# Layer 0 of a four-layer graph network: where x, the row sums and the loads of the adjacency matrix are placed

## The chip, the cores and the metric

The kernel runs on one core of a Trainium2 chip. A core has five engines that run their own instruction streams side by side and wait for each other by semaphores: TensorE (PE, matrix products, with its weight loads listed apart as PEld), VectorE (DVE), ScalarE (ACT), GpSimd (POOL) and SyncE (SP), which here only issues DMA transfers. Transfers are issued from an engine's queue (SP's or ACT's) and are carried out by 16 DMA engines. The metric is the time of one execution on the device in microseconds (us); lower is better.

## The reference, cut to what matters

There are N = 2708 nodes with D = 128 features, x[N, D], and a sparse weighted matrix adj[N, N] stored dense in float32 (29.3 MB). Four layers follow each other; each takes h = relu(layernorm(x)) and adds its output to x.

```
h = max(layernorm(x), 0)
layer 0:  x = x + (adj.T @ h) / adj.sum(axis=0)[:, None]
layer 1:  s, d = h @ Wa.T, h @ Wb.T
          x = x + ln(gelu([h, sum_j gelu(s_i + d_j + b) * adj_ij] @ U.T + u) + h)
layer 2:  x = x + gru(relu((adj @ h) @ W.T + b), h)
layer 3:  x = x + sum over 2 heads of elu(ln(softmax(masked scores) @ hh + h) @ F.T) / 2
```

Layer 1 would need a gelu for each of N x N pairs; the kernel does it only for the entries of adj that are not zero. For this it draws up lists in layer 0, while adj passes through the core.

## The kernel before, in words

*Tiles.* The 2708 rows are cut into 22 row tiles (NT) of 128, the last of 20. Row tiles are taken four at a time (GROUPS: five groups of 4 and one of 2). Columns are cut into 22 blocks (NB) of 124 for the lists.

*Start.* Lines 78 to 82 issue the loads of x from ACT's queue into xs, one transfer per group. `normalise` (L140, called at L157) runs for each group: `moments` (L109) on VectorE takes mean and variance of each row, GpSimd takes the power -1/2 (L119), `factors` (L122) makes one Newton step and the shift on VectorE, and `scale_rows` (L132) writes h on ScalarE. Constants for layer 1 follow (L174 to L191, L199): count, ident_h, before, xb and offdiag.

*Layer 0* (L197 to L258) loops over groups, and in a group over its row tiles:

- The buffer `a4` holds four row tiles; there are two of them, so group g + 2 needs the buffer of group g. Each row tile has a load of its own on SP's queue (L218).
- TensorE multiplies h of the row tile with its six column chunks into six PSUM banks, which collect over all row tiles (L220).
- GpSimd copies the columns near the diagonal into `near` without the diagonal, and the diagonal alone into `dg` (L229 to L232). VectorE sums `dg` into `own` (L235).
- VectorE takes for each of the 22 column blocks the eight largest entries of every row and their positions (L240, L241). These are the lists.
- ScalarE counts the entries of a row as the sum of their signs (L243).
- After a group's row tiles, TensorE transposes them, four 128 x 128 blocks into one PSUM bank (L249, two banks); ScalarE copies the bank to `aT` and sums it (L253: `sums` gives the column sums of adj); SP stores `aT` to a transposed copy of adj in DRAM (L256), which layer 2 and layer 3 read. There are four `aT` buffers.

At the end ScalarE copies the six banks to sumT (L258), and VectorE makes the inverse column sums (L263 to L267).

*What sets the order.* In layer 0 a scheduler orders each engine's instructions; each engine then takes its own strictly in that order, and so does SP with its transfers: a load that waits for a buffer holds back the stores behind it. From layer 1 on the order is written out by hand. Layer 1 opens on VectorE with count_rows (L333), rank (L349), the inverse sums and `enter` (L656), which adds layer 0's result to x.

*Weights.* `load`, `load_columns` and `load_rows` (L87 to L103) issue the weights of layers 1 to 3 from ACT's queue. gate_b and half_b (L276 to L279) are made on VectorE ahead of layer 1; `layer3_weights` (L286) runs in layer 2.

Of the kernel before, what the change touches and what calls it, by code (L numbers as in the profile page):

```python
# [20 lines left out]
F32 = mybir.dt.float32  # L21
BF16 = mybir.dt.bfloat16
AF = mybir.ActivationFunctionType
ALU = mybir.AluOpType
# [36 lines left out]
def listed_layers(ctx: ExitStack, tc: tile.TileContext, x, adj, w, out, flag):  # L61
# [14 lines left out]


    nc.vector.memset(xs[:, NT - 1, :], 0.0)
    for t, k in GROUPS[:-1]:
        nc.scalar.dma_start(xs[:, t : t + k, :], x[t * P : (t + k) * P, :].rearrange("(t p) d -> p t d", p=P))  # L80
    nc.scalar.dma_start(xs[:, FULL - 1, :], x[(FULL - 1) * P : FULL * P, :])
    nc.scalar.dma_start(xs[0:TAIL, FULL, :], x[FULL * P : N, :])

    ident = const.tile([P, P], F32, name="ident")
    make_identity(nc, ident)

    def load(pool, name, shape=None):  # L87
        t = pool.tile(list(shape or w[name].shape), F32, name=name)
        nc.scalar.dma_start(t, w[name])
        return t  # L90

    def load_columns(pool, name):

        k = w[name].shape[0] // P
        t = pool.tile([P, k], F32, name=name)
        nc.scalar.dma_start(t, w[name].rearrange("(k p) -> p k", p=P), allow_slow_non_contiguous=True)
        return t

    def load_rows(pool, name):

        t = pool.tile([P, w[name].shape[0]], F32, name=name)
        nc.scalar.dma_start(t, w[name].partition_broadcast(P))
        return t  # L103


    minus_half = const.tile([P, 8], F32, name="minus_half")
    nc.vector.memset(minus_half, -0.5)

    def moments(src, name, pool=small):  # L109
# [22 lines left out]
    def scale_rows(dst, src, rstd, shift, func):  # L132

        for q in range(len(src)):
            nc.scalar.activation(dst[q], src[q], func, bias=shift[:, q : q + 1], scale=rstd[:, q : q + 1])

    def tiles_of(v, t, k):
        return [v[:, t + q, :] for q in range(k)]

    def normalise(dst, src, t, k, func, name):  # L140

        rows = tiles_of(src, t, k)
        scale_rows(tiles_of(dst, t, k), rows, *factors(*moments(rows, name)), func)
# [10 lines left out]
        n = span(first, k)[1]  # L154
        (copy or nc.vector.tensor_copy)(dst, p[:, 0:n])

    for t, k in GROUPS:  # L157
        normalise(h, xs, t, k, AF.Relu, "n0")

    late = ctx.enter_context(tc.tile_pool(name="late", bufs=1))  # L160
    lists = ExitStack()
# [12 lines left out]
    count = keep.tile([P, P], F32, name="count")  # L174
    nc.gpsimd.iota(count, [[1, P]], base=0, channel_multiplier=0, allow_small_or_imprecise_dtypes=True)
    count_h = keep.tile([P, P], BF16, name="count_h")
    nc.vector.tensor_copy(count_h, count)
    ident_h = keep.tile([P, P], BF16, name="ident_h")
    nc.vector.tensor_copy(ident_h, ident)
    part = keep.tile([P, 1], F32, name="part")  # L180
    nc.gpsimd.iota(part, [[0, 1]], base=0, channel_multiplier=1, allow_small_or_imprecise_dtypes=True)
    before = keep.tile([P, P], BF16, name="before")
    nc.vector.tensor_scalar(before, count, part, None, ALU.is_gt)
    ends4 = keep.tile([P, NB, R], BF16, name="ends4")
    rows_n = keep.tile([P, NT, NB], BF16, name="rows_n")
    ends = keep.tile([P, NT, NB], BF16, name="ends")
# [1 line left out]
    nc.gpsimd.memset(later, 0.0)  # L188
    xb = [keep.tile([P, NB, C], BF16, name=f"xb{q}") for q in range(2)]
    for q in range(2):  # L190
        nc.vector.tensor_copy(xb[q][:, :, 4 * S : 4 * S + R], part.unsqueeze(1).to_broadcast([P, NB, R]))  # L191

# [2 lines left out]
    with tc.tile_pool(name="l0c", bufs=1) as fix:  # L197
        offdiag = fix.tile([P, P], F32, name="offdiag")
        nc.vector.tensor_scalar(offdiag, ident, -1.0, 1.0, ALU.mult, ALU.add)  # L199
        sums = fix.tile([P, NT, len(GROUPS)], F32, name="sums")  # L200
        nc.gpsimd.memset(sums, 1.0)
        with (
            tc.tile_pool(name="l0", bufs=2) as rows,
            tc.tile_pool(name="l0k", bufs=2) as pool,
            tc.tile_pool(name="l0t", bufs=4) as turned,
            tc.tile_pool(name="l0p", bufs=1, space=PSUM) as acc,
        ):
            accs = [acc.tile([P, CH], F32, name=f"acc{c}") for c in range(len(CHUNKS))]
            for gi, (g0, gk) in enumerate(GROUPS):
                i0, iw = span(g0, gk)  # L210
                a4 = rows.tile([P, 4, N], F32, name="a")
                if gk < 4:
                    nc.gpsimd.memset(a4[:, gk - 1, :], 0.0)
                for q in range(gk):
                    n = g0 + q
                    m = size(n)
                    a = a4[:, q, :]
                    nc.sync.dma_start(a[0:m, :], adj[n * P : n * P + m, :])  # L218
                    for ci, (c, cw) in enumerate(CHUNKS):
                        nc.tensor.matmul(  # L220
                            accs[ci][:, 0:cw], h[0:m, n, :], a[0:m, c : c + cw], start=(n == 0), stop=(n == NT - 1)
                        )

                    d0 = n * P
                    b0 = d0 // JB
                    b1 = (d0 + m - 1) // JB
                    c0, c1 = b0 * JB, min((b1 + 1) * JB, N)
                    near = pool.tile([P, 3 * JB], F32, name="near")
                    nc.gpsimd.tensor_copy(near[:, 0 : c1 - c0], a[:, c0:c1])  # L229
                    dg = pool.tile([P, P], F32, name="dg")  # L230
                    nc.gpsimd.tensor_tensor(dg[:, 0:m], a[:, d0 : d0 + m], ident[:, 0:m], ALU.mult)
                    nc.gpsimd.tensor_tensor(  # L232
                        near[:, d0 - c0 : d0 - c0 + m], a[:, d0 : d0 + m], offdiag[:, 0:m], ALU.mult
                    )
                    nc.vector.reduce_sum(own[:, n : n + 1], dg[:, 0:m], AX.X)  # L235
                    for b in range(NB):
                        ab = a[:, b * JB : b * JB + width(b)]
                        if b0 <= b <= b1:
                            ab = near[:, b * JB - c0 : b * JB - c0 + width(b)]
                        nc.vector.max(val[:, n, b, :], ab)  # L240
                        nc.vector.max_index(col[:, n, b, :], val[:, n, b, :], ab)  # L241
                    sign = pool.tile([P, N], BF16, name="sign")
                    nc.scalar.activation(sign, a, AF.Sign, accum_out=total[:, n : n + 1])  # L243
                for j in range(NT):
                    k = size(j)
                    p = bank("p_T")
                    for q in range(gk):
                        m = size(g0 + q)
                        nc.tensor.transpose(  # L249
                            p[0:k, q * P : q * P + m], a4[0:m, q, j * P : j * P + k], ident[0:m, 0:m]  # L250
                        )
                    aT = turned.tile([P, CH], F32, name="aT")
                    nc.scalar.activation(  # L253
                        aT[0:k, 0:iw], p[0:k, 0:iw], AF.Copy, accum_out=sums[0:k, j, gi : gi + 1]
                    )
                    nc.sync.dma_start(adjT[0:k, j, i0 : i0 + iw], aT[0:k, 0:iw])  # L256
            for ci, (c, cw) in enumerate(CHUNKS):
                nc.scalar.copy(sumT[:, c : c + cw], accs[ci][:, 0:cw])  # L258


        deg = fix.tile([P, 3, NT], F32, name="deg")
        dsum, lim, fin = (deg[:, q, :] for q in range(3))
        nc.vector.reduce_sum(dsum, sums, AX.X)  # L263
        nc.vector.reciprocal(inv, dsum)
        nc.vector.tensor_scalar(lim, inv, FMAX, -FMAX, ALU.min, ALU.max)
        nc.vector.tensor_tensor(fin, lim, inv, ALU.is_equal)
        nc.vector.tensor_tensor(inv, lim, fin, ALU.mult)  # L267
# [5 lines left out]
    attn = load_columns(late, "attn")  # L273
    gain1, shift1, gain2, shift2 = (load_columns(late, v) for v in ("g1", "b1", "g2", "b2"))
    gate_b = late.tile([P, 2], F32, name="gate_b")
    nc.vector.tensor_tensor(gate_b, b_ih[:, 0:2], b_hh[:, 0:2], ALU.add)  # L276
    nc.vector.tensor_scalar(gate_b, gate_b, 0.5, None, ALU.mult)
    half_b = late.tile([P, 1], F32, name="half_b")
    nc.vector.tensor_scalar(half_b, b_hh[:, 2:3], 0.5, None, ALU.mult)  # L279


    NX = 2 * D + 4
    w_x = late.tile([P, NX], F32, name="w_x")
    src_w = late.tile([P, 2, P], F32, name="src_w")

    def layer3_weights():  # L286
        nc.vector.tensor_copy(w_x[:, 0 : 2 * D], ff0T)
        for k in range(2):
            p = bank("p_w")[:, 0:2]
            nc.tensor.matmul(p, ff0[:, k, :], attn[:, 2 * k : 2 * k + 2], start=True, stop=True)  # L290
            nc.vector.tensor_copy(w_x[:, 2 * D + k : 2 * D + k + 1], p[:, 1:2])
            nc.vector.tensor_copy(w_x[:, 2 * D + 2 + k : 2 * D + 3 + k], p[:, 0:1])
        for k in range(2):
            nc.vector.tensor_copy(src_w[:, k, :], w_x[:, 2 * D + 2 + k : 2 * D + 3 + k].to_broadcast([P, P]))
# [639 lines left out]
    with (  # L934
# [127 lines left out]
        for g, (t0, k0) in enumerate(GROUPS):  # L1062
            pa = accs.tile([P, CH], F32, tag=f"acc{g % 2}", name="p_agg")
            for j0 in range(0, NT, PIECE):
                aggregate(t0, k0, pa, j0)
            if t0 == 0:
                layer3_weights()
            follow(finish_chunk(t0, k0, pa))
            advance()
        last = RUNS[0]  # L1070
# [486 lines left out]
```

## Time and profile before

| | |
|---|---|
| time, median of 3 runs | 1110.71 us (1109.0 to 1111.08) |
| span of the profiled execution | 1108.1 us, mean granted TensorE clock 0.933 |
| busy: PE, DVE, ACT, POOL | 963.6, 839.4, 504.2, 394.1 us |
| layer 0: first adj load issued, last list entry | 0.7 us, 244.3 us |
| layer 0, 28 to 244 us: busy PE, DVE, ACT, POOL | 178.2, 215.6, 135.3, 27.6 us |
| moved in this stretch | 237 GB/s, DMA share 0.68 |
| layer 1 opens with L656 at | 246.85 us |

How to read the profile lines: a line of the order of time gives start, length, engine, line of the kernel, operation, what it writes and reads with shapes, how many were merged, and in brackets the idle time before it and what ended it. A line of the waits says who waited for whom: total us, number of times, the longest. A line of the stretches gives busy us per engine with the number of instructions, then the granted clock (1.00 is full speed), the DMA share and GB/s. Busy times of TensorE are pipelined matmuls, so they overstate its work. Adding busy times up over the kernel says little here, since its layers have different limits: layer 0 has to be looked at by itself.

### The profile page before, as it was taken

What the parts mean: (1) busy time and instruction counts of PE and PEld (TensorE: products, weight loads), DVE (VectorE), ACT (ScalarE), POOL (GpSimd) and SP (SyncE); (2) the same over time, 40 slices, a digit from 0 to 9 for tenths busy, and PEclk for the clock granted to TensorE, in tenths of its full rate; (3) what the DMA queues carried; (4) which work ended last, traced back from release to release, by engine and by line L of the source; (5) the groups of instructions that cost most, each with busy time, mean ns of one, the idle gap of its engine ahead of it and who ended that gap; (6) DMA issues with size and microseconds to landing.
All of it is one profiled execution on the core that took longest, in us unless ns stands there. A gap on an engine that the chain in (4) does not pass through costs nothing. (4 is left out here: it accounts for less than half of the span.)

```text
span 1108.1 us, 21904 instructions
## 1 busy us (share of the span) xinstructions
PE 963.6 (87%) x7968; PEld 760.1 (69%) x7968; DVE 839.4 (76%) x2948; ACT 504.2 (46%) x1319; POOL 394.1 (36%) x466
## 2 busy tenths in 40 slices
PE   3998887944389999999999979999979999999993
PEld 1455444523389999999898934444468899999772
DVE  5999999997766668676887255655578977997673
ACT  3857556623476666656676521433322200230142
POOL 4111111103385655776566253344310200340132
PEclk9999889755699999999999989999989999999996
DMA  9488978522133222322222056545300000000000
GB/s 361 164 299 281 324 259 288 178 64 68 46 106 102 96 86 90 106 86 101 83 103 80 28 193 209 190 157 198 100 18 1 1 9 1 1 20 1 2 15 14
DMA packets 55298, 125.39 MB, mean 113 GB/s; under 512 B 7414, under 2 KB 19782, under 8 KB 52472
## 3 DMA queue, kind: packets, MB, share of 16 engines
q1 hardware_dynamic: 48590, 121.12, 31.6%
q10 hardware_dynamic: 6590, 2.77, 1.0%
q8 instruction: 64, 1.05, 0.4%
q14 instruction: 54, 0.44, 0.1%
HBM read 77.30 MB, written 30.84 MB: 98 GB/s over the span
## 5 line engine op out<-in xcount | busy, mean ns | idle before, releaser
L838 PE MATMUL att<-hv,wt 128*128 128x129 f32 (+2 forms) x1936 | 240.7, 281 | 9.2 <-DVE wt L806 9.2
L838 PEld LDWEIGHTS att<-hv,wt 128*128 128x128 f32 (+2 forms) x1936 | 221.8, 190 | 26.2 <-DVE wt L806 9.1
L806 DVE SCALAR_TENSOR_TENSOR wt<-row,lift,mask 128x1024 f32<-128x1024 f32 (+5 forms) x176 | 160.0, 939 | 34.2 <-PE att L838 34.2
L423 POOL TENSOR_SCALAR put<-mine,value 128x128 f32<-128x128 bf16 x176 | 147.7, 855 | 72.4 <-DVE mine L339 70.0
L499 PE MATMUL p_m<-s,sel 128*128 128x128 bf16 x1452 | 160.8, 219 | 5.4 <-ACT g L511 5.4
L119 POOL TENSOR_TENSOR n_r<-n_r,minus_half 128x4 f32<-128x4 f32 (+1 forms) x36 | 51.3, 1425 | 316.1 <-DVE n_r L118 305.2
L503 PE MATMUL p_m<-d,cols 124*128 124x128 bf16 (+1 forms) x1452 | 161.0, 219 | 1.4 <-DVE cols L453 1.3
L220 PE MATMUL acc<-a,hs 128*128 128x512 f32 (+2 forms) x264 | 122.3, 599 | 27.6 <-DMA a<-in_adj 18.9
L524 PE MATMUL agg<-put,g 128*128 128x128 f32 (+1 forms) x968 | 135.8, 281 | 0.0
L241 DVE FIND_INDEX8 col<-val,a 128x8 uint16<-128x124 f32 (+1 forms) x441 | 118.6, 280 | 0.0
L959 PE MATMUL p_agg<-a,hs 128*128 128x512 f32 (+2 forms) x264 | 111.5, 564 | 7.7 <-DVE u L572 4.8
L524 PEld LDWEIGHTS agg<-put,g 128*128 128x128 f32 x968 | 118.1, 192 | 0.0
L499 PEld LDWEIGHTS <-sel 128*128 128x128 bf16 x1452 | 103.7, 97 | 10.8 <-issue 7.1
L503 PEld LDWEIGHTS <-cols 124*128 124x128 bf16 (+1 forms) x1452 | 101.8, 97 | 1.9 <-DVE cols L453 1.9
L240 DVE MAX8 val<-a 128x8 f32<-128x124 f32 (+1 forms) x441 | 102.6, 272 | 0.0
L511 ACT ACTIVATE g<-p_m 128x512 f32<-128x512 f32 x132 | 73.0, 553 | 63.6 <-PE p_m L503 63.6
L431 ACT ACTIVATE put<-mine,value 128x128 f32<-128x128 bf16 x308 | 100.5, 390 | 0.0
L220 PEld LDWEIGHTS acc<-a,hs 128*128 128x128 f32 (+1 forms) x264 | 49.7, 209 | 72.2 <-issue 43.4
L249 PEld LDWEIGHTS p_T<-ident,a 128*128 128x128 f32 x484 | 59.0, 146 | 52.8 <-ACT aT L253 25.4
L249 PE MATMUL p_T<-ident,a 128*128 128x128 f32 x484 | 77.7, 293 | 18.3 <-DMA a<-in_adj 10.0
L253 ACT ACTIVATE aT<-p_T 128x512 f32<-128x512 f32 (+2 forms) x132 | 70.9, 541 | 40.0 <-issue 16.3
L959 PEld LDWEIGHTS p_agg<-a,hs 128*128 128x128 f32 (+1 forms) x264 | 48.6, 196 | 56.6 <-issue 55.1
(228 smaller groups left out, 1396.6 us busy)
## 6 DMA issues: line engine op xcount, KB each, us to landing
a<-in_adj SPq DMA_DIRECT2D x21, 1354.0 KB
adjT<-aT SPq DMA_DIRECT2D x105, 256.0 KB
a<-adjT SPq DMA_DIRECT2D x20, 1280.0 KB
spread<-passed SPq DMA_DIRECT2D x22, 704.0 KB
later<-sel SPq DMA_DIRECT2D x22, 616.0 KB
later<-sel SPq DMA_DIRECT2D x22, 82.5 KB
adjT<-aT SPq DMA_DIRECT2D x21, 74.0 KB
a<-adjT SPq DMA_DIRECT2D x4, 370.0 KB
```

Of the source, the lines that this page charges most:

```text
L220: nc.tensor.matmul(accs[ci][:, 0:cw], h[0:m, n, :], a[0:m, c : c + cw], start=(n == 0), stop=(n == NT - 1))
L240: nc.vector.max(val[:, n, b, :], ab)
L241: nc.vector.max_index(col[:, n, b, :], val[:, n, b, :], ab)
L249: nc.tensor.transpose(p[0:k, q * P : q * P + m], a4[0:m, q, j * P : j * P + k], ident[0:m, 0:m])
L423: nc.gpsimd.tensor_scalar(st["put", 0][:, b, :], st["mine"][:, b, :], st["value"][:, b : b + 1], None, ALU.mult)
L431: nc.scalar.activation(st["put", 1][:, b - HP, :], st["mine"][:, b, :], AF.Identity, scale=st["value"][:, b : b + 1])
L499: nc.tensor.matmul(p[:, b - b0, :], st["sel"][:, b, :], s3[:, q, t % 2, :], start=(q == 0), stop=False)
L503: nc.tensor.matmul(p[:, b - b0, :], st["cols"][0:kb, b, :], d3[0:kb, b, q, :], start=False, stop=(q == 2))
L524: nc.tensor.matmul(agg, g[:, b - 4 * k, :], put, start=(b == 0), stop=False)
L806: nc.vector.scalar_tensor_tensor(wt[0:kj, :], row[0:kj, k, c : c + n], lift[0:kj, j, k : k + 1], mask[0:kj, j, c : c + n], op0=ALU.max, op ...
L838: nc.tensor.matmul(banks[s // 3][0:m, s % 3, :], wt[0:kj, q * P : q * P + m], hv[0:kj, j, k, :], start=(v < 2 and s // 3 not in touched), ...
L959: nc.tensor.matmul(pa[:, 0:n], h[0:k, j, :], a[0:k, j - j0, 0:n], start=(j == 0), stop=(j == NT - 1))
```

## The change

The change rearranges layer 0; nothing of what is computed changes.

1. The first four row tiles of x are loaded ahead of adj on SP's queue; the other 18 follow after the second row tile of adj (`load_rest`). All weights go to SP's queue as well.
2. Only the first four tiles are normalised as before. For the others `moments_apart` takes the moments on ScalarE, by a Copy and a Square, each with a sum over its columns, and makes the factors on GpSimd for all 18 tiles together.
3. The sum of the diagonal, `own`, goes from VectorE to ScalarE.
4. Groups 1 to 4 are loaded by one transfer for four row tiles; the first and the last group keep one for each row tile. There are eight `aT` buffers.
5. Constants of layer 1 are made on GpSimd; gate_b and half_b are made later, in layer 2.

It is meant to start VectorE's lists sooner, to leave VectorE nothing but the lists, and to issue fewer transfers.

```diff
-    for t, k in GROUPS[:-1]:
-        nc.scalar.dma_start(xs[:, t : t + k, :], x[t * P : (t + k) * P, :].rearrange("(t p) d -> p t d", p=P))
-    nc.scalar.dma_start(xs[:, FULL - 1, :], x[(FULL - 1) * P : FULL * P, :])
-    nc.scalar.dma_start(xs[0:TAIL, FULL, :], x[FULL * P : N, :])
+    nc.sync.dma_start(xs[:, 0:4, :], x[0 : 4 * P, :].rearrange("(t p) d -> p t d", p=P))
+    def load_rest():
+        for t, k in GROUPS[1:-1]:
+            nc.sync.dma_start(xs[:, t : t + k, :], x[t * P : (t + k) * P, :].rearrange("(t p) d -> p t d", p=P))
...
-    for t, k in GROUPS:
-        normalise(h, xs, t, k, AF.Relu, "n0")
+    normalise(h, xs, 0, 4, AF.Relu, "n0")
...
-    nc.vector.tensor_copy(count_h, count)
+    nc.gpsimd.tensor_copy(count_h, count)
...
+        def moments_apart(pool):
+            for t in range(4, NT):
+                junk = pool.tile([P, D], F32, name="junk")
+                nc.scalar.activation(junk, xs[:, t, :], AF.Copy, accum_out=shifts[:, t - 4 : t - 3])
+            nc.gpsimd.tensor_scalar(shifts, shifts, -1.0 / D, None, ALU.mult)
+            for t in range(4, NT):
+                junk = pool.tile([P, D], F32, name="junk")
+                nc.scalar.activation(
+                    junk, xs[:, t, :], AF.Square, bias=shifts[:, t - 4 : t - 3], accum_out=ve[:, t - 4 : t - 3]
+                )
+            nc.gpsimd.tensor_scalar(ve, ve, 1.0 / D, EPS, ALU.mult, ALU.add)
+            nc.gpsimd.tensor_tensor(rstd, ve, minus_half[:, 0:RT], ALU.pow)
...
+            scale_rows(tiles_of(h, 4, RT), tiles_of(xs, 4, RT), rstd, shifts, AF.Relu)
...
-            tc.tile_pool(name="l0t", bufs=4) as turned,
+            tc.tile_pool(name="l0t", bufs=8) as turned,
...
-                    nc.sync.dma_start(a[0:m, :], adj[n * P : n * P + m, :])
+                    if not 0 < gi < len(GROUPS) - 1:
+                        nc.sync.dma_start(a[0:m, :], adj[n * P : n * P + m, :])
+                    elif q == 0:
+                        nc.sync.dma_start(a4, adj[i0 : i0 + iw, :].rearrange("(t p) n -> p t n", p=P))
+                    if n == 1:
+                        load_rest()
...
-                    nc.vector.reduce_sum(own[:, n : n + 1], dg[:, 0:m], AX.X)
...
+                    if n == 2:
+                        moments_apart(pool)
                     sign = pool.tile([P, N], BF16, name="sign")
                     nc.scalar.activation(sign, a, AF.Sign, accum_out=total[:, n : n + 1])
+                    nc.scalar.activation(dg[:, 0:m], dg[:, 0:m], AF.Copy, accum_out=own[:, n : n + 1])
...
-    def layer3_weights():
+    def late_weights():
+        nc.vector.tensor_tensor(gate_b, b_ih[:, 0:2], b_hh[:, 0:2], ALU.add)
```

More of the change, by code (lines that the diff above doesn't have):

```diff
@@ L78, in listed_layers @@
     nc.vector.memset(xs[:, NT - 1, :], 0.0)
-    for t, k in GROUPS[:-1]:
-        nc.scalar.dma_start(xs[:, t : t + k, :], x[t * P : (t + k) * P, :].rearrange("(t p) d -> p t d", p=P))
-    nc.scalar.dma_start(xs[:, FULL - 1, :], x[(FULL - 1) * P : FULL * P, :])
-    nc.scalar.dma_start(xs[0:TAIL, FULL, :], x[FULL * P : N, :])
+    nc.sync.dma_start(xs[:, 0:4, :], x[0 : 4 * P, :].rearrange("(t p) d -> p t d", p=P))
+    def load_rest():
+        for t, k in GROUPS[1:-1]:
+            nc.sync.dma_start(xs[:, t : t + k, :], x[t * P : (t + k) * P, :].rearrange("(t p) d -> p t d", p=P))
+        nc.sync.dma_start(xs[:, FULL - 1, :], x[(FULL - 1) * P : FULL * P, :])
+        nc.sync.dma_start(xs[0:TAIL, FULL, :], x[FULL * P : N, :])
     ident = const.tile([P, P], F32, name="ident")
@@ L88, in load @@
         t = pool.tile(list(shape or w[name].shape), F32, name=name)
-        nc.scalar.dma_start(t, w[name])
+        nc.sync.dma_start(t, w[name])
         return t
@@ L95, in load_columns @@
         t = pool.tile([P, k], F32, name=name)
-        nc.scalar.dma_start(t, w[name].rearrange("(k p) -> p k", p=P), allow_slow_non_contiguous=True)
+        nc.sync.dma_start(t, w[name].rearrange("(k p) -> p k", p=P), allow_slow_non_contiguous=True)
         return t
@@ L101, in load_rows @@
         t = pool.tile([P, w[name].shape[0]], F32, name=name)
-        nc.scalar.dma_start(t, w[name].partition_broadcast(P))
+        nc.sync.dma_start(t, w[name].partition_broadcast(P))
         return t
-    minus_half = const.tile([P, 8], F32, name="minus_half")
+    minus_half = const.tile([P, NT], F32, name="minus_half")
     nc.vector.memset(minus_half, -0.5)
@@ L176, in listed_layers @@
     count_h = keep.tile([P, P], BF16, name="count_h")
-    nc.vector.tensor_copy(count_h, count)
+    nc.gpsimd.tensor_copy(count_h, count)
     ident_h = keep.tile([P, P], BF16, name="ident_h")
-    nc.vector.tensor_copy(ident_h, ident)
+    nc.gpsimd.tensor_copy(ident_h, ident)
     part = keep.tile([P, 1], F32, name="part")
@@ L182, in listed_layers @@
     before = keep.tile([P, P], BF16, name="before")
-    nc.vector.tensor_scalar(before, count, part, None, ALU.is_gt)
+    nc.gpsimd.tensor_scalar(before, count, part, None, ALU.is_gt)
     ends4 = keep.tile([P, NB, R], BF16, name="ends4")
@@ L190, in listed_layers @@
     for q in range(2):
-        nc.vector.tensor_copy(xb[q][:, :, 4 * S : 4 * S + R], part.unsqueeze(1).to_broadcast([P, NB, R]))
+        nc.gpsimd.tensor_copy(xb[q][:, :, 4 * S : 4 * S + R], part.unsqueeze(1).to_broadcast([P, NB, R]))
     sumT = keep.tile([D, N], F32, name="hT1")
@@ L201, in listed_layers @@
         nc.gpsimd.memset(sums, 1.0)
+        RT = NT - 4
+        flat = fix.tile([P, 4, RT], F32, name="flat")
+        shifts, ve, rstd, tmp = (flat[:, q, :] for q in range(4))
+        def moments_apart(pool):
[10 more added lines that the diff above has]
+            nc.gpsimd.tensor_tensor(rstd, ve, minus_half[:, 0:RT], ALU.pow)
+            nc.gpsimd.tensor_tensor(tmp, rstd, rstd, ALU.mult)
+            nc.gpsimd.tensor_tensor(tmp, tmp, ve, ALU.mult)
+            nc.gpsimd.tensor_scalar(tmp, tmp, -0.5, 1.5, ALU.mult, ALU.add)
+            nc.gpsimd.tensor_tensor(rstd, rstd, tmp, ALU.mult)
+            nc.gpsimd.tensor_tensor(shifts, shifts, rstd, ALU.mult)
+            scale_rows(tiles_of(h, 4, RT), tiles_of(xs, 4, RT), rstd, shifts, AF.Relu)
         with (
@@ L275, in listed_layers @@
     gate_b = late.tile([P, 2], F32, name="gate_b")
-    nc.vector.tensor_tensor(gate_b, b_ih[:, 0:2], b_hh[:, 0:2], ALU.add)
-    nc.vector.tensor_scalar(gate_b, gate_b, 0.5, None, ALU.mult)
     half_b = late.tile([P, 1], F32, name="half_b")
-    nc.vector.tensor_scalar(half_b, b_hh[:, 2:3], 0.5, None, ALU.mult)
     NX = 2 * D + 4
@@ L284, in listed_layers @@
     src_w = late.tile([P, 2, P], F32, name="src_w")
-    def layer3_weights():
+    def late_weights():
+        nc.vector.tensor_tensor(gate_b, b_ih[:, 0:2], b_hh[:, 0:2], ALU.add)
+        nc.vector.tensor_scalar(gate_b, gate_b, 0.5, None, ALU.mult)
+        nc.vector.tensor_scalar(half_b, b_hh[:, 2:3], 0.5, None, ALU.mult)
         nc.vector.tensor_copy(w_x[:, 0 : 2 * D], ff0T)
@@ L1066, in listed_layers @@
             if t0 == 0:
-                layer3_weights()
+                late_weights()
             follow(finish_chunk(t0, k0, pa))
```

## The prediction

> **What bounds the kernel now.** I read the busy time by stretch first. Its columns are the stretch, its length, the busy time of TensorE, weight loads, VectorE, ScalarE and GpSimd, the granted clock, the DMA share and GB/s.
>
> ```profile
> 0.00:20.00 20.00, 1.35 (x4) 0.58 (x4) 9.12 (x59) 4.37 (x5) 7.71 (x16) 1.00 0.96 336
> 60.00:100.00 40.00, 35.54 (x156) 21.13 (x155) 40.00 (x271) 24.28 (x56) 4.68 (x11) 0.96 0.90 303
> 140.00:180.00 40.00, 33.31 (x136) 19.05 (x135) 40.00 (x272) 24.62 (x54) 5.20 (x12) 0.91 0.76 267
> 220.00:244.00 24.00, 11.48 (x40) 6.50 (x40) 24.00 (x164) 7.84 (x42) 0.50 (x2) 0.56 0.26 72
> ```
>
> VectorE is busy without a gap from 32 us to 244 us; no other engine is. Then its order of time: when it starts, when the per-block maxima start, when they end.
>
> ```profile
> 11.05 0.49 DVE L116 BATCH_NORM_STATS2 n_st<-xs 128x6 f32<-128x128 f32 x2 [10.04 <-DMA xs<-in_x]
> 16.55 2.07 DVE L127 TENSOR_SCALAR n_r<-n_r 128x4 f32<-128x4 f32 x3
> 21.38 0.28 DVE L240 MAX8 val<-a 128x8 f32<-128x124 f32 x1
> 244.04 0.26 DVE L241 FIND_INDEX8 col<-val,near 128x8 uint16<-128x104 f32 x1
> 246.85 1.13 DVE L656 SCALAR_TENSOR_TENSOR xs<-p_m,inv_deg,xs 128x128 f32<-128x128 f32 x4
> ```
>
> The first x group lands only at 11 us, the maxima start at 21.4, and layer 1 opens at 246.85 (L656), 2.5 us after the last maximum. ScalarE's order of time and the sync queue's show how near the second chain is: load of four row tiles, transposes (TensorE), evacuations aT (ScalarE), stores, next load.
>
> ```profile
> 141.10 0.58 ACT L253 ACTIVATE aT<-p_T 128x512 f32<-128x512 f32 x1
> 142.88 0.60 ACT L253 ACTIVATE aT<-p_T 128x512 f32<-128x512 f32 x1 [0.54 <-ACT aT L253]
> 144.62 0.60 ACT L253 ACTIVATE aT<-p_T 128x512 f32<-128x512 f32 x1 [0.47 <-ACT aT L253]
> 192.32 2.46 ACT L243 ACTIVATE sign<-a 128x2708 bf16<-128x2708 f32 x1 [2.83 <-DMA a<-in_adj]
> 233.49 0.28 ACT L253 ACTIVATE aT<-p_T 20x148 f32<-20x148 f32 x1
> 67.46 0.33 SPq L218 DMA_DIRECT2D a<-in_adj  x1
> 185.52 0.33 SPq L218 DMA_DIRECT2D a<-in_adj  x1
> ```
>
> The chain ends at 233.7, 10.5 us before VectorE. So that is all that VectorE's relief can bring before the chain sets the end, unless the chain moves too. The waits confirm it: the first two lines are GpSimd waiting for VectorE (free), the last two the chain waiting for loads.
>
> ```profile
> POOL near L229 <- DVE col L241: 92.6, 19, 9.3
> POOL dg L231 <- DVE own L235: 74.4, 18, 7.5
> ACT sign L243 <- DMA a<-in_adj: 28.8, 11, 5.0
> PE acc L220 <- DMA a<-in_adj: 18.9, 9, 4.3
> ```
>
> **What the Trainium skill says.** "ScalarE: Activation LUTs", What ACT_TABLE_LOAD costs: an ACTIVATE takes 186 ns + 0.833 ns a column, 93 ns more for each pointer operand, and neighbours overlap by 93 ns. The trace agrees: two pointers on 128 columns make 479 ns, hs measures 483; one makes 386, gs measures 394. "TensorE: Matmul & The Clock Gate", Part 1: after an idle window of about 3.4 us the clock is halved until a busy one. The trace agrees: eight matmuls took 6.42 us after 4.3 us of waiting, 3.70 us after 1.65. "DMA: Bandwidth & Descriptors", Queues, rings and completion order: the engines take turns between the queues by packet. It fits: x, on the other queue beside adj, landed at 11 us though issued at 0.7. "SBUF — State Buffer", two separate sides: a GpSimd operation and a VectorE operation in a two-port mode lock each other out. It fits the 2.07 us at L127, beside the 2.44 us memset of GpSimd; maxima beside GpSimd's near and dg keep their pace.
>
> **The change part by part.**
>
> *VectorE.* Two pairs of maximum and index take 0.89 us (236.25 to 237.14), so 484 pairs take 215.4. Before, from 21.38 to 244.3 there lie 222.9: 215.4, 22 sums own at 0.2 (4.4), and the rest of the norm (3). Afterwards sums, constants and the norm of 18 tiles are gone. Tile 0 lands at about 7.5: it landed at 7.18 with x beside it, now 0.26 MB of x goes ahead of it. In the compiled order the maxima follow the four tiles' statistics at once. End: 7.5 + 215.4 + 1.5 for small operations = 224.4, if no load is late; a lock by GpSimd's memset adds at most 2.4.
>
> *ScalarE's start.* It now carries the moments. A Copy with sum over 128 columns costs 293 - 93 + 93 for the read of the sum = 0.29 us; bounds are 0.2 (read hidden) and 0.5 (hs pace 0.41 plus 0.1). A sum own costs the same, a Square with a bias 0.38. I take the page's prices, since 148 columns with a sum measure a step of 0.285. Order: sign 0 to 10.0; hs, two own, sign 1, with 1 us of waiting for GpSimd's constants, to 16.5; 18 Copies (5.2) to 21.7; sign 2 to 24.2; 18 Squares (6.8) to 31; own and sign 3 to 33.8; GpSimd's power over 18 columns (0.70 for 2, 1.01 for 4, hence 3.2) and six small ones, 2 of it not hidden, to 36; 18 hs at 0.41 to 43.3. Only then the evacuations: four signs (9.8), four own (1.2), 20 aT. Pairs between signs take 1.2, a row of them 0.75 each (142.88, 144.62, 146.10): 4.8 + 9 = 13.8. The buffer of group 0 is free at R0 = 68, against 67.5 before. VectorE had left it at 47: the gain waits here.
>
> *Four tiles per load.* In the compiled order each load stands where the first of four stood, behind 20 of the 22 stores, so VectorE, TensorE and GpSimd must have left the buffer; two stores and the next group's queue up behind it. A group is 5.55 MB; between 20 and 32 us the trace moves 0.425 MB/us, hence 13.1 us. A single tile landed 8.0, 7.1, 7.3 and 6.8 us after issue, 4 more than its 3.3: stores ahead and latency. So 17 us, bounds 15.5 and 19. ScalarE in the meantime does six aT (eight buffers allow it) and then stands before the sign. After landing: four signs 9.8, own 1.2, 14 aT 9.3, and 1 us as TensorE is cold after 10 us of idling: 21.3. A cycle is 38.3 (before: 40.1, 37.5, 40.4, where tiles came in between stores). Landings at 85, 123, 162; VectorE leaves the groups at 86.7, 126, 165. It doesn't starve, by 2 to 4 us. R3 = 68 + 3 x 38.3 = 183.
>
> *Tail.* Before, from the load of tile 20 to the last aT it took 48.2 us. Four aT that ran in the wait now come after it (+3), while four more buffers remove most of the stop behind tile 21's load (two gaps, 4.4). I take 47, bounds 45 and 51. The chain ends at 230; TensorE's cold stretches may add some, so 231. The first step of layer 1 waits for TensorE and ScalarE too, so the 2.5 us to L656 follow, less 0.26 for gate_b and half_b. L656 at 233.5 to 235, against 246.85: 12 to 13 us. I take 12.
>
> *At no cost.* Constants on GpSimd: its 11 us gap before 12.7 hides them. Weights on the sync queue: about 1 MB, issued while DMA stood idle (36 to 44 us), some stores behind them, buffers enough. Later gate_b and half_b: three of 0.14 us in layer 2. The wider minus_half lies under the x load. From L656 on the order of all engines is the same, so the gain is carried whole.
>
> **Rivals.**
> - *VectorE still ends last*: 224.4 + 2.3 = 226.7, 20 less: 1090.5. For it: the chain could keep up, having waited on VectorE's release before. Against: it needs a tail of 41, which the four added aT forbid.
> - *The load's wait takes the place of VectorE, slower*: sums at 0.5 (R0 = 75), loads of 19 and 23 after them (42 a cycle), tail 50: 75 + 126 + 50 = 251, L656 at 253.3, 1117. For it: ScalarE and TensorE stand idle for each whole load, and the clock halves; granted clock 0.83 and 0.56 at the end of layer 0 now. Against: six aT run in the wait, and the prices of ScalarE agree with its rows.
> - *No change*: cycle 41, tail 49, R0 = 71: 243, L656 at 245.5, so 1109.5.
>
> **How the numbers follow.** The forecast (the chain ends layer 0 at about 231) has 0.66, VectorE last 0.13, no change 0.08, slower 0.13. Time: 1110.7 - 12 = 1098.7. The range takes in the first rival at 1089.5 and goes up to 1109.5, where the unknown costs (R0 +3, cycle +1.5, tail +3, together 10.5) put the forecast; left out are the slow case and some of the faster. Faster by over 0.2% (2.2 us): 0.66 + 0.13, and 0.01 of the third case, 0.80; within: 0.07; slower: 0.13.
>
> **What would show it.** The first maximum at 7 to 9 us; VectorE done at 223 to 228 and then idle until about 231, where before it never waited. Hs of tile 21 at 43; single loads of a group issued at about 68, 106 and 145, landing 17 later; Copies of 0.29. L656 at about 234, the rest shifted whole. It would be wrong if the sums cost 0.5, if a group took over 20 us to land, so that VectorE waits between groups, or if layer 1's opening loses what it was given.

## The result, and the profile after

The changed kernel takes 1098.17 us (median of 4 runs, 1097.69 to 1098.31), the kernel before 1110.76 us (median of 4 runs made beside them): a ratio of 0.9889, 95% interval 0.9872 to 0.9906. The forecast was 1098.7.

The busy time by stretch of the changed kernel, with the stretches and columns that the prediction shows for the kernel before:

```profile
0.00:20.00 20.00, 9.81 (x22) 4.66 (x23) 14.01 (x94) 13.40 (x48) 9.62 (x25) 1.00 0.94 348
60.00:100.00 40.00, 30.85 (x142) 18.47 (x141) 40.00 (x273) 24.93 (x60) 4.90 (x12) 0.87 0.78 295
140.00:180.00 40.00, 32.76 (x145) 19.20 (x144) 40.00 (x272) 25.31 (x65) 4.95 (x12) 0.91 0.74 279
220.00:244.00 24.00, 14.14 (x49) 8.06 (x49) 13.25 (x68) 9.35 (x47) 3.73 (x5) 0.56 0.46 143
```

VectorE (third busy time) works 14 us of the first 20, not 9, and in the middle it is still never idle. The last stretch is new: 13.25 of 24 us. VectorE's order of time says why:

```profile
7.53 0.48 DVE L269 MAX8 val<-a 128x8 f32<-128x124 f32 x2 [2.24 <-DMA a<-in_adj]
...
223.21 0.28 DVE L270 FIND_INDEX8 col<-val,near 128x8 uint16<-128x104 f32 x1
233.39 0.25 DVE L365 TENSOR_SCALAR some<-val 128x176 bf16<-128x176 f32 x1 [9.90 <-ACT aT L285]
...
235.76 1.12 DVE L688 SCALAR_TENSOR_TENSOR xs<-p_m,inv_deg,xs 128x128 f32<-128x128 f32 x4
```

The lists start 13.9 us earlier and end 20.8 us earlier, at 223.5. Then VectorE stands idle for 9.9 us until the last aT of ScalarE is made, and layer 1 opens at 235.76 in place of 246.85: 11.1 us earlier, not 21. So ScalarE, not VectorE, now ends layer 0. These lines are the sync queue's loads of groups 2 to 4 and of tile 20, and then ScalarE's sign that waits for the first of them:

```profile
68.70 0.38 SPq L246 DMA_DIRECT2D a<-in_adj  x1
...
107.38 0.38 SPq L246 DMA_DIRECT2D a<-in_adj  x1
...
146.86 0.38 SPq L246 DMA_DIRECT2D a<-in_adj  x1
...
185.59 0.33 SPq L244 DMA_DIRECT2D a<-in_adj  x1
```

```profile
86.03 2.46 ACT L274 ACTIVATE sign<-a 128x2708 bf16<-128x2708 f32 x1 [8.96 <-DMA a<-in_adj]
```

Each group's sign starts 17.3 to 17.7 us after its load is issued (86.03, 125.04, 164.24), and ScalarE stands idle for 7 to 9 us before it. It has 16 aT of the previous group left at that moment, and the next load is issued only when nearly all of these are done.

From L688 on the rest is nearly the same, but not quite. The last VectorE operation of the program ends at 1089.95 us, before at 1100.28: 10.3 us earlier, so 0.8 of the 11.1 is missing there. The span ends 5.9 us after it, before 7.8. So 11.1 - 0.8 + 1.9 = 12.2 us, the difference of the two spans (1095.9 and 1108.1).

### The profile page after: what moved, and what is told of

The parts are those of the page before. It is cut to its first block, busy times and chain, and to the rows that moved or that the text cites. A ratio compares the mean times of both kernels' runs of the same rounds, so it can differ in the third digit from the quotient of the medians.

```text
span 1095.9 us, 21907 instructions
## 1 busy us (share of the span) xinstructions
PE 965.2 (88%) x7968; PEld 762.9 (70%) x7968; DVE 825.4 (75%) x2855; ACT 520.7 (48%) x1435; POOL 396.3 (36%) x474
## 5 line engine op out<-in xcount | busy, mean ns | idle before, releaser
L121 POOL TENSOR_TENSOR n_r<-n_r,minus_half 128x4 f32<-128x4 f32 (+1 forms) x31 | 46.5, 1501 | 314.9 <-DVE n_r L120 304.1
L250 PE MATMUL acc<-a,hs 128*128 128x512 f32 (+2 forms) x264 | 118.7, 588 | 25.9 <-DMA a<-in_adj 22.2
L531 PEld LDWEIGHTS <-sel 128*128 128x128 bf16 x1452 | 104.0, 97 | 10.9 <-issue 7.1
L281 PEld LDWEIGHTS p_T<-ident,a 128*128 128x128 f32 x484 | 61.4, 151 | 57.6 <-ACT aT L285 33.0
L281 PE MATMUL p_T<-ident,a 128*128 128x128 f32 x484 | 80.4, 302 | 19.8 <-DMA a<-in_adj 10.2
L285 ACT ACTIVATE aT<-p_T 128x512 f32<-128x512 f32 (+2 forms) x132 | 71.0, 544 | 31.7 <-issue 13.9
```

The source lines that it names most:

```text
L250: nc.tensor.matmul(accs[ci][:, 0:cw], h[0:m, n, :], a[0:m, c : c + cw], start=(n == 0), stop=(n == NT - 1))
L281: nc.tensor.transpose(p[0:k, q * P : q * P + m], a4[0:m, q, j * P : j * P + k], ident[0:m, 0:m])
L531: nc.tensor.matmul(p[:, b - b0, :], st["sel"][:, b, :], s3[:, q, t % 2, :], start=(q == 0), stop=False)
```

## The experiments

All kernels here compute what the two kernels compute; they differ in the order, engines and buffers of layer 0, and experiments 9 and 12 in the queue of one weight load. Each ratio is to runs of the kernel before that were made beside it. Differences in microseconds to the changed kernel compare runs made at different times, over which the kernel before moved by 1.2 us (medians of 1109.52 to 1110.76). "Enter" is the operation that opens layer 1 (L656 in the kernel before, L688 in the changed one), and "aT ends" means the end of the last aT. Theory A is that of the prediction, taken one step further: ScalarE's chain (load, sign, aT, release, next load) now ends layer 0, and it is long because ScalarE stands idle before a sign whose load is in flight, while aT are left to do.

**1. The order on ScalarE.** Signs of a group stand behind the last aT of the group before.

```diff
-                    nc.scalar.activation(sign, a, AF.Sign, accum_out=total[:, n : n + 1])
-                    nc.scalar.activation(dg[:, 0:m], dg[:, 0:m], AF.Copy, accum_out=own[:, n : n + 1])
+                    with tc.issue_after(last_aT.ins) if gi > 0 else ExitStack():
+                        nc.scalar.activation(sign, a, AF.Sign, accum_out=total[:, n : n + 1])
+                        nc.scalar.activation(dg[:, 0:m], dg[:, 0:m], AF.Copy, accum_out=own[:, n : n + 1])
```

> Only the order on ScalarE changes: the signs and diagonal sums of a group of four row tiles stand behind the last aT of the group before, so ScalarE never stands before a load with evacuations left that would release a buffer. Theory A (in the changed kernel the end of layer 0 is set by the chain load, sign, aT, release, load, and the chain is long because ScalarE stands 7 to 9 us per group before the first sign of a group in flight): the releases come some 16 us earlier, loads hide, VectorE ends last at 223.5 us, the first enter of layer 1 (L688, now at 235.8) stands at about 226, time 1088 to 1089. Theory B (the chain is long because of its own work, cold TensorE and evacuations, and moving the sign only moves the wait): L688 at 233 to 236, time 1096 to 1098.

Measured: 1094.45 us, ratio to the kernel before 0.9854 (0.9837 to 0.9872); enter is at 232.9. Neither theory has the number. The loads come earlier, at 62.9, 95.5 and 126.1, but the fourth only at 168.1, and aT ends at 230.8. The wait had moved, as two lines of this kernel's waits tell:

```profile
ACT dg L276 <- POOL dg L261: 19.7, 3, 10.4
...
DVE some L366 <- ACT aT L286: 7.1, 1, 7.1
```

ScalarE's diagonal sum needs dg of GpSimd; GpSimd makes dg after near, and near has two buffers which VectorE reads. Once ScalarE runs ahead, this ties it to VectorE's pace. Experiment 5 tests that.

**2. One load for each row tile again.**

```diff
-                    if not 0 < gi < len(GROUPS) - 1:
-                        nc.sync.dma_start(a[0:m, :], adj[n * P : n * P + m, :])
-                    elif q == 0:
-                        nc.sync.dma_start(a4, adj[i0 : i0 + iw, :].rearrange("(t p) n -> p t n", p=P))
+                    nc.sync.dma_start(a[0:m, :], adj[n * P : n * P + m, :])
```

> Undoes one part: one load for each row tile of adj again, in all groups. In the compiled order the loads of tiles 8 to 15 then stand behind the stores of group 1 too. Theory A (the time of a group's load lies on the chain): the first sign of a group need not wait for four tiles; but tile 8 is issued only at about 85 us, lands at 92, VectorE waits some 6 us for it once and then runs through to about 229: L688 at 231 to 232, time 1093 to 1095. Theory C (four tiles in one load is what lets VectorE run without a wait, single loads starve it at every group): VectorE waits at groups 2 to 5, L688 after 238, time over 1100.

Measured: 1093.62 us, ratio 0.9846 (0.983 to 0.9863); enter at 232.8. VectorE waits once, at tile 8, and then runs through to 230.4:

```profile
93.70 0.48 DVE L266 MAX8 val<-a 128x8 f32<-128x124 f32 x2 [6.86 <-DMA a<-in_adj]
```

As theory A said; theory C falls. The four-tile load is no part of the gain: with the rest of the change it costs 4.5 us (1098.17 - 1093.62; the enters of the profiled runs are 3.0 apart). With single loads aT ends at 230.7, together with the lists.

**3. Diagonal sums on VectorE again.**

```diff
+                    nc.vector.reduce_sum(own[:, n : n + 1], dg[:, 0:m], AX.X)
...
-                    nc.scalar.activation(dg[:, 0:m], dg[:, 0:m], AF.Copy, accum_out=own[:, n : n + 1])
```

> Undoes one part: the 22 diagonal sums own are on VectorE again (0.2 us each, 4.4 in all), off ScalarE (0.29 each, 6.4). Theory A (ScalarE's chain ends layer 0, VectorE has 10 us to spare): VectorE ends at about 228, the chain gives back 1.2 us in each of the three cycles and about as much ahead of them, 4 to 5 us in all; L688 at about 231, time 1093 to 1094. Theory D (VectorE's relief is what made the change faster): 4 us slower, 1102.

Measured: 1090.70 us, ratio 0.9835 (0.9804 to 0.9866); 7.5 us faster than the changed kernel, though VectorE has 4.4 us more to do. The lists end at 227.5 (VectorE had room), aT ends at 223.8 in place of 233.65, and enter follows VectorE at 229.75. Theory A has the direction, and was too small: the chain gives back 9.9 us, not 4 to 5. From the group loads (66.4, 105.0, 143.1, 181.0) it is 2.3 ahead of the first release, 2.3 in the three cycles, and 5.3 behind the last load. The sums themselves are 22 x 0.29 = 6.4, but only two of them (0.6) lie behind the last load. Most of the 5.3 there is therefore not the sums' own time. TensorE's granted clock from 204 to 220 us was 0.88 in this run, against 0.68 in the changed kernel; that this is the reason was not tried. Theory D falls.

**4. Moments of the 18 later tiles on VectorE again.**

```diff
-                        moments_apart(pool)
+                        for t, k in GROUPS[1:]:
+                            normalise(h, xs, t, k, AF.Relu, "n0")
```

> Undoes one part: the moments of the 18 later tiles of x are on VectorE again (about 9 us with their small operations), off ScalarE, whose 36 sums (12 us) stood ahead of the first evacuations. Theory A: the first release comes 10 to 12 us earlier (at 57 instead of 68.7, VectorE needs its group until about 56), the chain ends at about 223, VectorE at about 232.5: L688 at about 235, time 1097 to 1098, so no difference to the changed kernel. Theory D (VectorE's relief made the gain): slower by 9, 1107. Theory E (the sums on ScalarE are hidden, so nothing is won back there): slower as well, 1100 or more.

Measured: 1108.85 us, ratio 0.9989 (0.9982 to 0.9996). Theory A missed by 11 us. VectorE ends its lists at 235, 11.5 later, but it is not last: aT ends at 245.7, and VectorE still stands 10.2 us for it. The first release comes not at 57 but at 74.2. I had taken the moments as VectorE time alone; they are a relay. Scheduled among the lists, each group's moments go VectorE, GpSimd (power), VectorE (shift), ScalarE (h), and the first and last line of these waits of this kernel show two of the hand-overs:

```profile
POOL n_r L121 <- DVE n_r L120: 24.5, 5, 16.9
...
ACT dg L276 <- POOL dg L261: 10.6, 5, 3.4
...
ACT hs L137 <- DVE n_r L131: 8.3, 5, 4.3
```

The last h is made at 53 us, 11 later than in the changed kernel. The line between is the tie of experiment 1: with VectorE later, ScalarE's diagonal sums stand for it. Against the changed kernel the first release is 5.5 us later, the cycles 0.9 longer, the part behind the last load 5.7 longer: the 12.1 between the two enters. Of the 5.7 us, 3.0 are one such wait, for the sum of tile 20. So the moments were worth moving, though not for 9 us of VectorE, which were there to spare. The relay explains the late first release; the rest of the last part (2.7 us) stays open. Theories D and E both have the sign of it; D has the number, but by VectorE ending last, which it doesn't.

**5. The order of experiment 1, and five buffers for near and dg.**

```diff
+            tc.tile_pool(name="l0n", bufs=5) as npool,
...
-                    near = pool.tile([P, 3 * JB], F32, name="near")
+                    near = npool.tile([P, 3 * JB], F32, name="near")
...
-                    dg = pool.tile([P, P], F32, name="dg")
+                    dg = npool.tile([P, P], F32, name="dg")
```

> The order of the first experiment (signs of a group behind the last aT of the group before), and near and dg in a pool of their own with five buffers in place of two. In the first experiment ScalarE stood 19.7 us, three times, before the diagonal sum for dg of GpSimd, which stood before near's buffer, which VectorE held. Theory A2 (that wait, a tie of ScalarE to VectorE through two buffers, is what kept the first experiment from its 1088): it is gone, aT ends before VectorE, VectorE ends last at 223.5, L688 at 226, time 1086 to 1088. Theory B (TensorE's and ScalarE's own work at the end, cold): aT still ends at 229 or later, time 1093 to 1095.

Measured: 1086.36 us, ratio 0.9789 (0.9773 to 0.9805). ScalarE's wait for dg is gone, aT ends at 218.6, and the lists are followed at once by layer 1:

```profile
223.04 0.27 DVE L271 FIND_INDEX8 col<-val,near 128x8 uint16<-128x104 f32 x1
223.22 0.25 DVE L367 TENSOR_SCALAR some<-val 128x176 bf16<-128x176 f32 x1
...
225.58 1.12 DVE L690 SCALAR_TENSOR_TENSOR xs<-p_m,inv_deg,xs 128x128 f32<-128x128 f32 x4
```

Against the changed kernel's lines above: same end of the lists, no 9.9 us wait, enter 10.2 us earlier. This version beats both kernels; it is 23 us under the kernel before. Theory B falls: TensorE stays at half clock from 186 us on (0.50 in the stretches to 220), and it costs nothing.

**6 and 7. Four aT buffers, and twelve, in place of eight.** Two, six or ten aT stand ahead of a group's first sign.

```diff
-            tc.tile_pool(name="l0t", bufs=8) as turned,
+            tc.tile_pool(name="l0t", bufs=4) as turned,
```

> Undoes one part: four aT buffers, as in the kernel before, in place of eight. In the compiled order only two aT then stand ahead of the first sign of a group, and 20 come after the landing. Theory A (ScalarE stands through the rest of each load, and each aT that doesn't fit ahead of the sign is paid after it): 4 x 0.7 to 0.75 in each of three cycles, 8 to 9 us: aT ends at about 242, L688 at 244, time 1105 to 1107. Theory F (VectorE hides it, or the buffers do nothing): within 2 us of the changed kernel, 1097 to 1100.

> The other way: twelve aT buffers in place of eight; ten aT stand ahead of the first sign of a group. Theory A: the chain gives back about 2.8 us in each of three cycles, aT ends at 225 to 227, about with VectorE: L688 at 227.5 to 229, time 1089 to 1091. Theory F (buffers do nothing): 1097 to 1099.

Measured: with four 1109.12 us, ratio 0.9995 (0.9985 to 1.0004), no faster than the kernel before; with twelve 1088.54 us, ratio 0.9801 (0.9783 to 0.9819). Group loads: 68.2, 110.7, 152.1, 195.9 with four, 68.4, 103.7, 139.4, 176.6 with twelve. So three cycles take 127.8, 116.9 (the changed kernel) and 108.2 us with two, six and ten aT ahead: 10.9 and 8.7 us for four aT, where 8 to 9 were expected. With four, ScalarE's waits for loads grow from 35.4 to 43.6 us, and VectorE waits 15.2 us for the last aT and 8.2 for loads (9.9 and 2.2 in the changed kernel):

```profile
DVE some L365 <- ACT aT L285: 15.2, 1, 15.2
...
DVE val L269 <- DMA a<-in_adj: 8.2, 3, 4.3
```

VectorE now starves between groups too. The profiled run with twelve is the longest of its four, 1092.25; aT ends there at 228, and enter is at 230.3. Theory F falls on both sides: without the four added buffers, the change is worth nothing that these runs show.

**8. The order of the loads alone** (with the weights on the sync queue, the constants on GpSimd and the later gate_b and half_b): moments and diagonal sums on VectorE, one load for each tile, four aT buffers. Its edit is that of experiments 2, 3, 4 and 6 together.

> Only the order of the loads (first rows of x ahead of adj, the rest of x behind its second tile, weights on the sync queue) and the constants on GpSimd; moments and diagonal sums on VectorE, one load for each tile, four aT buffers, as before. The maxima start at 7.5 instead of 21.4, but moments of the later tiles now lie between them. VectorE: 7.5 + 215.4 + 4.4 + 9 + 2 = 238 if it ends last: L688 at 240.5, time 1103 to 1104, about half of the gain. Rival (as in the fourth experiment, late factors of hs hold up ScalarE and the first release comes at 72 or later): the chain ends last at 242 or later, 1105 to 1110.

Measured: 1103.55 us, ratio 0.9939 (0.9922 to 0.9955). The time is that of the first theory, the reason half: the lists end at 239.1, near the 238 worked out, then VectorE waits 2.8 us for aT, and enter is at 244.3 in the profiled run, itself 1105.37. Of the 4.5 us between its span (1103.6) and that of the kernel before, 2.6 come from the earlier enter, 0.2 from the layers behind it and 1.7 from the end of the program, which experiments 9 and 12 take up. VectorE's first moments start 7.3 us earlier than in the kernel before (3.74, before 11.05) and its lists end 5.2 us earlier, but the layer keeps only 2.6: the chain ends 3 us after VectorE.

**9. One 2 KB weight load on ScalarE's DMA queue again**, to explain the 1.9 us behind the last operation of VectorE.

```diff
-    attn = load_columns(late, "attn")
+    attn = late.tile([P, w["attn"].shape[0] // P], F32, name="attn")
+    nc.scalar.dma_start(attn, w["attn"].rearrange("(k p) -> p k", p=P), allow_slow_non_contiguous=True)
```

> The changed kernel with one 2 KB weight load (attn) on ScalarE's DMA queue again, all else the same. From the last VectorE operation (y) to the end of the span the kernel before took 7.8 us, the changed kernel and all others so far 5.8 to 6.1; the kernel before is the only one of them that used a second DMA queue. Theory Q (the end of the program takes longer for a second queue): the tail is 7.8 us again, time 1099.5 to 1100.5. Theory N (the tail depends on something else, for instance on what ran before): tail 5.9, time 1098 to 1098.5.

Measured: 1097.25 us, with runs from 1095.25 to 1104.34, ratio 0.9914 (0.988 to 0.9949). The end took 8.5 us from the last VectorE operation, as theory Q said, but the time didn't rise: enter came at 233.7, 2.0 us before that of the changed kernel, with the same order of instructions. The stretch from 204 to 220 us tells them apart, first the changed kernel, then this one:

```profile
204.00:220.00 16.00, 15.30 (x70) 10.85 (x69) 16.00 (x109) 11.62 (x35) 0.45 (x3) 0.68 0.55 210
```

```profile
204.00:220.00 16.00, 15.40 (x84) 9.42 (x82) 16.00 (x109) 14.67 (x48) 0.64 (x3) 0.99 0.68 257
```

The granted clock is 0.68 in one and 0.99 in the other, and ScalarE is busy 14.7 us in place of 11.6. From the sign of tile 20 to the end of aT it takes 40.7 us in the changed kernel and 37.2 here; ahead of that sign this run is 1.4 us later. As time this run is inconclusive on the queue; experiment 12 repeats it where VectorE ends the layer, some us after the chain.

**10. The order of experiment 1 in the kernel before.**

> The kernel before with the order of the first experiment alone (signs of a group behind the last aT of the group before). Theory A (before the change VectorE ends layer 0 last and the chain only has to keep up, so an earlier chain is worth nothing): last maximum at 244, L656 at 246.5 to 247, time 1109 to 1111. Theory G (the order is a gain of its own): 1100 to 1105.

Measured: 1110.71 us, ratio 1.0012 (1.0005 to 1.0019); last list at 244.2, enter at 246.83. The number is theory A's, and G falls, but the chain did not become earlier: aT ends at 243.8, in the kernel before at 233.8. What this shows is less than I asked: ten us more on the chain cost next to nothing (0.1%) while VectorE ended last. That an earlier chain is worth nothing there was not tried.

**11. Five buffers for near and dg alone**, in the changed kernel.

> The changed kernel with near and dg in a pool of five buffers alone. Theory A2: in the changed kernel VectorE runs ahead of ScalarE, so near's buffers are free in time, and the ScalarE chain is what ends last: aT ends at 233 to 234, time 1097.5 to 1098.5, no difference. Theory H (the buffers of near are a limit of their own): 1094 or less.

Measured: 1098.42 us, ratio 0.9903 (0.9886 to 0.9919), enter at 235.86: no difference, as A2 said. The changed kernel's ScalarE waits for dg only 0.6 us. The buffers are worth something only once the order lets ScalarE run ahead.

**12. The kernel of experiment 5 with the load of experiment 9.**

> The kernel of the fifth experiment (VectorE ends layer 0 last, so TensorE's clock can't move the end of the layer) with one 2 KB weight load on ScalarE's DMA queue, all else the same. Theory Q (a second DMA queue costs about 2 us at the end of the program): from the last VectorE operation to the end of the span 7.8 to 8.5 us in place of 5.9, time 1088 to 1089 against 1086.4. Theory N: no difference, 1086 to 1087.

Measured: 1089.00 us, ratio 0.9818 (0.9802 to 0.9834), 2.6 us over experiment 5. Enter is 0.65 later, but the last VectorE operation ends 0.2 us earlier; it is the end that is longer, 8.5 us in place of 5.9. Theory Q holds. In this kernel the second queue moved so little that the profile rounds it to 0.00 MB:

```profile
q10 hardware_dynamic: 528, 0.00, 0.0%
```

It is still paid for at the end.

**All profiled runs side by side** (us from the start of the span; the time is the median of all runs):

| kernel | lists end | aT ends | enter | time |
|---|---|---|---|---|
| before | 244.3 | 233.8 | 246.85 | 1110.76 |
| changed | 223.5 | 233.65 | 235.8 | 1098.17 |
| 1, signs last | 223.4 | 230.8 | 232.9 | 1094.45 |
| 2, tile loads | 230.4 | 230.7 | 232.8 | 1093.62 |
| 3, own sums back | 227.5 | 223.8 | 229.75 | 1090.70 |
| 4, moments back | 235.3 | 245.7 | 247.8 | 1108.85 |
| 5, signs last, five near and dg | 223.3 | 218.6 | 225.6 | 1086.36 |
| 6, four aT | 229.1 | 244.6 | 246.7 | 1109.12 |
| 7, twelve aT | 223.4 | 228.2 | 230.3 | 1088.54 |
| 8, loads alone | 239.1 | 242.2 | 244.3 | 1103.55 |
| 9, two queues | 223.9 | 231.6 | 233.7 | 1097.25 |
| 10, before, signs last | 244.2 | 243.8 | 246.8 | 1110.71 |
| 11, five near and dg alone | 223.3 | 233.8 | 235.9 | 1098.42 |
| 12, as 5, two queues | 224.0 | 216.8 | 226.2 | 1089.00 |

In each of them enter follows the later of the two ends by 2.1 to 2.6 us.

## Why the prediction was right, step by step

- *VectorE.* Lists from 7.5 to 223.5, against 7.5 to 224.4. 216 us for 484 pairs, with one wait of 2.2 us ahead of the first; VectorE doesn't starve.
- *ScalarE's start.* In the changed kernel a Copy with its sum steps by 0.29 us (15.01 to 15.30), a Square by 0.385 (22.71 to 23.09), which is what the prices of the Trainium skill's page "ScalarE: Activation LUTs", What ACT_TABLE_LOAD costs, give together with the 93 ns that the prediction added for the read of the sum. The last h is done at 41.9 (forecast 43.3), the first release is at 68.7 (68).
- *The load.* 17.3, 17.7 and 17.4 us from issue to the sign (17); from the sign to the next load 21.35, 21.8 and 21.35 (21.3); cycles 38.7, 39.5 and 38.7 (38.3). The last load issues at 185.6 (183): 2.6 of drift, of which 0.7 were there at the first release and 1.2 came in the second cycle. The 0.75 for an aT in a row was read too low: of the two steps shown, 1.74 and 1.48 for two aT, only the shorter gives it, and in the changed kernel two take 1.74 to 1.87. The 1 us set aside for a cold TensorE covered that.
- *Tail.* 48.1 (47, and 1 more for a cold TensorE). The chain ends at 233.65 (231), L688 at 235.8 (233.5 to 235). The chain was forecast 2.6 us short, and that is the drift ahead of the last load, not the tail. The tail's length is not the program's alone: from the sign of tile 20 on, experiment 9 takes 3.5 us less with the same order.
- *TensorE's clock.* The two groups of matmuls that the prediction shows for its rule of the clock agree with it, but two others of the same trace took 5.40 and 5.24 us after waits of 1.87 and 2.14 us, and one 3.70 after 1.96. The wait just before them does not decide it alone.
- *Carried whole.* As far as the runs show, yes. From enter to the last VectorE operation the changed kernel takes 854.2 us and the kernel before 853.4, but this stretch, whose work is the same in all kernels but for where gate_b and half_b are made, lies between 852.4 and 854.5 in the twelve experiments, so the 0.8 is not clear of their scatter. What was left out is the 1.9 us won behind the last operation since one queue is left. That the weights on the sync queue would save at the end of the program was no step of mine; I had costed that edit at nothing. So the mechanism was right, and that the total meets 12 so closely is luck: an enter that was 1 us worse, 0.8 us lost on the way and an end that was 2 us better than I said cancel.
- *Own sums.* 1.2 us a cycle was, if anything, too much: without the sums three cycles are 2.3 us shorter, 0.8 each. The 9.9 us that experiment 3 takes off the chain lie for the larger part at its start (2.3) and in its tail (5.3), and the tail's part is not explained by two sums.
- *The rivals.* VectorE last at 1090.5 is what experiments 3 and 5 make of it (1090.70, 1086.36), and my reason against it, a tail too long for it, held. The slower case has its parts in experiment 6: fewer aT in the wait, cycles of 42 to 44 us, VectorE starving. Even that came only to 1109.12, the number of the third rival, no change, and not to 1117. The changed kernel is four buffers away from it.

What the change gained, then: the lists start earlier and VectorE carries nothing else (20.8 us at the lists' end), of which the chain let 11.1 through. What held back the rest is shown by taking it away (experiment 5): the order of signs before aT and the tie through near's two buffers. Not each part of the change pays: the four-tile loads and the own sums on ScalarE made it slower with the rest in place (experiments 2 and 3), while without the moments' move or the aT buffers nearly nothing is left of the gain (experiments 4 and 6).

## What to carry to other kernels

When the busiest engine is relieved, work out when the second chain ends before counting the gain, and let its slack be the bound; then ask which single instruction of the chain stands in order before a load in flight while the work that frees the next buffer is queued behind it. Fixing that order and the buffers beside it gave nearly as much again as the whole change (11.8 us by the medians, 11.2 between the profiled spans, experiment 5). Work moved to an idle engine brings its inputs along: a sum on ScalarE that reads what GpSimd writes behind VectorE's buffers ties the three together.

## What the runs showed of the hardware that was not expected

- With ScalarE's DMA queue in use beside the sync queue, the end of the program is longer: from the last VectorE operation to the end of the span 7.8 to 8.5 us in the four kernels with two queues (the kernel before and experiments 9, 10 and 12), 5.8 to 6.1 in the ten with one. Experiments 5 and 12 differ in one 2 KB load only and are 2.7 us apart there. No other queue was tried as the second.
- TensorE's clock does not drop at the same moment in each run. In the changed kernel it is at half (0.50) from about 206 to 216 us although TensorE is busy 15.3 of the 16 us from 204 to 220; in experiment 9, with the same order, it is full until about 219. The Trainium skill's page "TensorE: Matmul & The Clock Gate", Part 1, tells of a drop after an idle window. The changed kernel's trace shows no such window ahead of the drop: its TensorE is busy 11.66 of the 12 us from 194 to 206. In experiment 9 it stood 3.3 us for the load of tile 20 and was slowed right then (0.70 from 194 to 198), but not at 206. What decides between them stays open.
